# One written-out order on all five engines for the attention of two batches

## The chip, the cores and the metric

The kernel runs on one core of a Trainium2 chip. A core has five engines that work at the same time, each with an instruction list of its own that it takes in order: TensorE (matrix products, PE), VectorE (DVE), ScalarE (ACT, activation functions and copies), GpSimd (POOL) and SyncE (SP, which here only issues transfers). ACT and POOL issue transfers too. An instruction waits for semaphores that other engines or transfers raise; while it waits, everything behind it on its list waits as well. All transfers share 16 DMA engines. The metric is device time in microseconds (us); all data is float32.

## The reference

Four batches of 512 tokens with 512 channels pass through an attention block and a feed-forward block, each behind a layer norm whose shift, scale and output gate come from a small modulation product.

```python
mod = (silu(c) @ wmod).reshape(4, 6, 1, 512)
sa, ca, ga, sb, cb, gb = (mod[:, i] for i in range(6))
ga, gb = ...                                  # sign kept, magnitude at least 0.25
h = layernorm(x) * (1 + ca) + sa
x = x + ga * attention(h)
h = layernorm(x) * (1 + cb) + sb
x = x + gb * ((silu(h @ w_gate.T) * (h @ w_up.T)) @ w_down.T)   # 2048 hidden channels

def attention(h):                             # 6 heads, key size 64, value size 128
    q, k, v = (silu(conv4(h @ W)) for W in (Wq, Wk, Wv))        # causal, 4 taps
    beta = sigmoid(h @ Wb)
    g = -exp(A_log) * softplus(h @ Wa + dt_bias)
    q, k = l2norm(q) / 8, l2norm(k)
    for t in tokens:                          # gated delta rule, state S of 64 x 128 per head
        S = S * exp(g[t])
        S = S + outer(k[t], (v[t] - k[t] @ S) * beta[t])
        o[t] = q[t] @ S
    o = o * rsqrt(mean(o * o) + 1e-5) * norm_weight * silu(h @ Wg)
    return o @ Wo
```

## The kernel before

**Stages.** Tokens are cut into 4 tiles (`NT`) of 128 per batch, each of two chunks of 64. For each batch `normed_t` makes the normed, modulated and transposed input `ht` (DVE statistics and scaling, TensorE transposes, an ACT pass with shift and scale). Then come 18 projections per batch, 128 output channels each: 3 of keys, 3 of queries, 6 of values, 6 of gates. A projection is four accumulating products of 512 columns into one PSUM bank (each is two instructions in the trace, since the data is float32). Keys, queries and values go through `conv_silu` (L427): ACT copies the bank with the last tap's weight (L432), DVE adds three taps (L434), ACT applies silu (L438). Keys and queries are also squared (L444) and summed over channels by TensorE (`pn`, L450); values are transposed and scaled (`by_token`, L496); gates only get a silu. All four results are stored to DRAM (`kd`, `qd`, `vd`, `sd`) and read back later in another layout. `decays` and `stored` make the decay factors from two small products (`pab`, `pat`).

**The delta rule.** `triangles(b)` makes, for all chunks and heads of a batch at once, the inverse of the 32 x 32 unit triangles: 30 pairs of DVE instructions in a chain (L598, L602), results to DRAM as `td` and `ttd`. For each tile `operands` loads keys, queries, values and triangles, builds the matrices `l`, `yk` and `it` (TensorE into the bank pair `scratch`, DVE and ACT out of it), and `scan` carries the state over the two chunks: `pf` (L695), a copy on ACT (L700), `pm` (L704), copies on DVE and ACT (L711, L712). `finish` and `project` norm and gate the output, multiply with `wo` (L745), add the residual, store `xmid` and take the second norm; `turned` transposes it into `hf`, the input of `feed_forward`.

**The rest.** `modulation(j)` makes one of six modulation vectors. `weight_sums` makes sums of feed-forward weights, 16 times a load, four POOL instructions (L808 to L811) and a store from POOL's queue (L812), through one buffer. `feed_forward(b)` multiplies with these sums (L960) and with `w_down` (L847, L890).

**What sets the order.** The program text calls the stages one after the other, and a planner that is part of the framework moves instructions past each other on every engine, by its own estimates of cost, as far as data and buffers allow; for all but batch 0 it is told that the inverse chain is of low priority (`LATER`, L594). `lagging` (L413) and `between` put a few pieces later in the program text by hand. The text issues batch 0's projections, its triangles and its delta rule, then the keys and queries of batches 1 to 3 together, and so on; batch 2's triangles and both delta rules of batches 2 and 3 are issued beside the feed-forwards. PSUM has three banks tagged `fill` (projections), three tagged `seq` (delta rule and small products) and the pair `scratch`. SP issues nearly all loads and stores, ACT the stores of `kd`, `qd` and `sd`, POOL those of the weight sums and of the output gates.

Of the kernel before, what the change touches and what calls it, by code (L numbers as in the profile page):

```python
# [7 lines left out]

F32 = mybir.dt.float32
AF = mybir.ActivationFunctionType  # L10
ALU = mybir.AluOpType
# [26 lines left out]
def adaln_block(  # L38
# [119 lines left out]
    act.activation(warm, eps, AF.Silu)  # L158
    act.activation(sc_t[:, :, :B], c_in, AF.Silu)

    last, steps = [], []

    def between(i):

        if i % 2 and steps:
            steps.pop(0)()


    def after(t):

        pool.tensor_copy(t, last[0][:1, :1])

    def modulation_load(j):

        early = j < 2
        wm = pa_.tile([P, KD, D], F32, tag="ht" if early else "wm", bufs=3 if early else 1, name=f"wm{j}")
        if not early:
            after(wm[:1, 0, :1])
        (act if early else sp).dma_start(
            wm, w_mod[:, j * D : (j + 1) * D].rearrange("(k p) f -> p k f", p=P)  # L180
        )
        return j, wm

    def modulation(j, wm):

        pm = fill(f"pm{j}")
        for k in range(KD):
            pe.matmul(pm[k * S : (k + 1) * S, :], sc_t[:, k, :], wm[:, k, :], start=True, stop=True)
        part = pa_.tile([P, D], F32, tag="acc", bufs=4, name=f"part{j}")
        vec.tensor_copy(part, pm)  # L190
        if j in MOD:
            pt = fill(f"pmt{j}")[:, : KD * B].rearrange("p (t b) -> p t b", b=B)
            for t in range(KD):
                pe.matmul(pt[:, t, :], part[:, t * P : (t + 1) * P], fold[:, :B], start=True, stop=True)
            vec.tensor_scalar_add(mod_t[:, MOD[j]], pt, 1.0 if j in (1, 4) else 0.0)
            return
        pg = fill(f"pmg{j}")[:B, :]
        pe.matmul(pg, fold[:, :B], part, start=True, stop=True)
        val = pa_.tile([P, D], F32, tag="acc", bufs=4, name=f"val{j}")[:B]
        vec.tensor_copy(val, pg)  # L200
        mag = pa_.tile([P, D], F32, tag="acc", bufs=4, name=f"mag{j}")[:B]
# [4 lines left out]
        pool.dma_start(gate_d[j // 3], mag)  # L206
# [6 lines left out]
    def load_x(b):  # L213
        ts = []
        if b == 2:

            room = w1.tile([P, NT, D], F32, tag="hf", bufs=2, name=f"xt{b}")
        for c in range(NT):
            if b == 2:
                t = room[:, c, :]  # L220
            else:
                t = pa_.tile([P, D], F32, tag="xt", bufs=4, name=f"xt{b}_{c}")
            (act if b else sp).dma_start(t, x[b, c * P : (c + 1) * P, :])
            ts.append(t)
        return ts

    for j in (1, 0):
        modulation(*modulation_load(j))
    first_w = weight(w_k, 0, "k0_0")
    xts = load_x(0)  # L230
# [4 lines left out]
    for nm, src, n in (("k", conv_k, NP), ("q", conv_q, NP), ("v", conv_v, H)):  # L235
        cw[nm] = const.tile([P, n, TAPS], F32, name=f"conv_{nm}")
        sp.dma_start(cw[nm], src.rearrange("(n p) i -> p n i", p=P))
    neg_a = const.tile([P, H], F32, name="neg_a")
    sp.dma_start(neg_a, a_log.partition_broadcast(P))
    act.activation(neg_a, neg_a, AF.Exp)  # L240
    pool.tensor_scalar(neg_a, neg_a, -1.0, None, ALU.mult)
    dtb = const.tile([P, H], F32, name="dtb")
    sp.dma_start(dtb, dt_bias.partition_broadcast(P))
    nw = const.tile([P, 1], F32, name="nw")
    sp.dma_start(nw, norm_weight.rearrange("(p o) -> p o", o=1))
    for t in gd:
        for a in range(2):
            sp.dma_start(t[a, 0, :, :, 0:1], far)
# [30 lines left out]
    def normed_t(b, xts):  # L279

        ht = pa_.tile([P, KD, T], F32, tag="ht", bufs=3, name=f"ht{b}")
        mv = pa_.tile([P, NT, vec.BN_AGGR_DIM], F32, tag="mv", name=f"mv{b}")
        rstd = pa_.tile([P, NT], F32, tag="rstd", name=f"rstd{b}")
        for c in range(NT):
            statistics(pa_, xts[c], mv[:, c, :])
        act.activation(rstd, mv[:, :, 1], AF.Sqrt, bias=eps)
        vec.reciprocal(rstd, rstd)
        for c in range(NT):
            vec.tensor_scalar(
                xts[c], xts[c], mv[:, c, 0:1], rstd[:, c : c + 1], ALU.subtract, ALU.mult  # L290
            )
        for k in range(KD):
            pt = fill(f"pxt{b}_{k}")
# [6 lines left out]
        return ht  # L300

    def decays(bs, hts):
# [3 lines left out]
        pab = (seq if bs == [0] else fill)(f"pab{n}")  # L321
# [18 lines left out]
        pat = (seq if bs == [0] else fill)(f"pat{n}")  # L340
# [18 lines left out]
        act.activation(beta, pv[:, :, :, H : 2 * H].rearrange("p b c h -> p b h c"), AF.Exp, scale=-1.0)  # L359
        flat = [v.rearrange("p b h c -> p (b h c)") for v in (z, e, t, t2, s, beta)]  # L360
        fz, fe, ft, ft2, fs, fb = flat
        vec.tensor_scalar_add(fb, fb, 1.0)
        vec.reciprocal(fb, fb)


        vec.scalar_tensor_tensor(fe, fz, -1.0, fz, ALU.mult, ALU.max)
        act.activation(fe, fe, AF.Exp, scale=-1.0)
# [3 lines left out]
        vec.tensor_mul(ft2, ft, ft)  # L371
        vec.tensor_scalar_mul(fs, ft2, 1.0 / 17.0)
        for q in (15.0, 13.0, 11.0, 9.0, 7.0, 5.0, 3.0):
            vec.scalar_tensor_tensor(fs, fs, 1.0 / q, ft2, ALU.add, ALU.mult)
        vec.scalar_tensor_tensor(fs, fs, 1.0, ft, ALU.add, ALU.mult)
# [8 lines left out]
        return beta, lambda: stored(bs, m, n, gy, g, y)  # L384

    def stored(bs, m, n, gy, g, y):

        pd = (seq if bs == [0] else fill)(f"pd{n}")
# [10 lines left out]
        for i, b in enumerate(bs):  # L399
# [3 lines left out]
            pgt = (seq if bs == [0] else fill)(f"pgt{b}")  # L403
# [3 lines left out]
            act.dma_start(  # L407
                gd[b].rearrange("a g h c i -> (g h c) a i")[:, :, 1:],
                gyt.rearrange("p (a i) -> p a i", a=2),
            )  # L410

    tails, pending = [], []

    def lagging(tail=None, lag=2):

        if tail is not None:
            tails.append(tail)
        while len(tails) > (lag if tail is not None else 0):
            tails.pop(0)()

    def projected(w, ht, nm):
        pp = fill(f"pp_{nm}")
        for k in range(KD):
            pe.matmul(pp, w[:, k, :], ht[:, k, :], start=(k == 0), stop=(k == KD - 1))  # L424
        return pp

    def conv_silu(w, taps, col, ht, nm):  # L427

        pp = projected(w, ht, nm)
        acc = pa_.tile([P, T], F32, tag="acc", bufs=4, name=f"acc_{nm}")  # L430
        last[:] = [acc]
        act.activation(acc, pp, AF.Copy, scale=taps[:, col, TAPS - 1 : TAPS])  # L432
        for i in range(1, TAPS):
            vec.scalar_tensor_tensor(  # L434
                acc[:, i:], pp[:, : T - i], taps[:, col, TAPS - 1 - i : TAPS - i], acc[:, i:],
                ALU.mult, ALU.add,
            )
        act.activation(acc, acc, AF.Silu)  # L438
        return acc

    def squares(t, dst, p, scale, nm):

        sq = pa_.tile([P, T], F32, tag="sq", bufs=1, name=f"sq_{nm}")
        act.activation(sq, t, AF.Square)  # L444
# [10 lines left out]
    def keys(bs, hts):  # L455
        if bs == [0]:
            betas, store = decays(bs, hts)
        sk = {}
        for i, b in enumerate(bs):
            sk[b] = pa_.tile([P, H, NT], F32, tag=f"sk{i}", bufs=1, name=f"sk{b}")  # L460
        for p in range(NP):
            w = first_w if bs == [0] and p == 0 else weight(w_k, p, f"k{bs[0]}_{p}")
            for b in bs:
                n = f"k{b}_{p}"
                kt = conv_silu(w, cw["k"], p, hts[b], n)
                act.dma_start(kd[b][:, p, :], kt)
                lagging(lambda a=(kt, sk[b], p, 1.0, n): squares(*a))
            if p == 1 and bs != [0]:
                betas, store = decays(bs, hts)
            if p == (1 if bs == [0] else 2):  # L470
                store()
        def scalars():
            for i, b in enumerate(bs):
                act.activation(nk[b], sk[b], AF.Sqrt)
                pool.tensor_scalar(nk[b], nk[b], -1.0, None, ALU.mult)
                vec.reciprocal(sc[b], sk[b])
                vec.scalar_tensor_tensor(sc[b], sc[b], -1.0, betas[:, i], ALU.mult, ALU.mult)

        lagging(scalars)

    def queries(bs, hts):
        for p in range(NP):
            w = weight(w_q, p, f"q{bs[0]}_{p}")
            for b in bs:
                n = f"q{b}_{p}"
                qt = conv_silu(w, cw["q"], p, hts[b], n)
                act.dma_start(qd[b][:, p, :], qt)
                lagging(lambda a=(qt, eq[b], p, float(DK) * EPS, n): squares(*a))

    def values(bs, hts):  # L490
        for h in range(H):
            w = weight(w_v, h, f"v{bs[0]}_{h}")
            for b in bs:
                vt = conv_silu(w, cw["v"], h, hts[b], f"v{b}_{h}")
                lagging(lambda a=(b, h, vt): by_token(*a))
                between(h)  # L496

    def by_token(b, h, vt):
# [8 lines left out]
        sp.dma_start(vd[b][:, :, h, :].rearrange("c p v -> p c v"), v)  # L507

    def gates(bs, hts):
        for h in range(H):  # L510
            w = weight(w_g, h, f"g{bs[0]}_{h}")
# [609 lines left out]
```

## Time and profile before

| what | us |
|---|---|
| median of 3 runs | 1313.92 (1313.06 to 1315.52) |
| span of the profiled execution | 1315.2 |
| TensorE busy in it | 1234.9 |
| VectorE / ScalarE / GpSimd busy | 733.7 / 383.5 / 290.8 |
| first key product starts | 23.9 |
| last product of batches 0 and 1 up to the second norm | 537.6 |
| first product of the feed-forward | 522.0 |

Busy time counts instructions, overlaps within an engine once. PEclk is the share of TensorE's full clock that was granted; at half clock a product takes twice as long and still counts as busy. The chain of waits goes back from the last instruction to what released each step. "PE a <- ACT b: 9.7, 4, 5.8" says that TensorE waited 9.7 us in all, 4 times, at most 5.8, for b on ScalarE.

### The profile page before, as it was taken

Reading aid. Unit: us, or ns where it says so; the run is one execution under the profiler, and the core shown is the slowest. Engines: PE = TensorE matmul, PEld = TensorE weight load, DVE = VectorE, ACT = ScalarE, POOL = GpSimd, SP = SyncE. Lnnn points to the kernel's source line nnn. Section 1 sums busy time; section 2 is a strip of 40 time slices with the busy share of each in tenths; the row PEclk is TensorE's granted clock in tenths of the full one; section 3 lists DMA queues with packets and bytes.
Section 4 is the critical chain, followed back from the end, with each engine's and each line's share of the span. In section 5 each row is a group of like instructions: output and inputs, shape, how many; then the busy total and the mean of one; then the engine's idle time right before and its main releaser. Section 6 shows DMA issues by size and latency. Waiting matters only on the chain.

```text
span 1315.2 us, 18413 instructions
## 1 busy us (share of the span) xinstructions
PE 1234.9 (94%) x6752; PEld 807.1 (61%) x6752; DVE 733.7 (56%) x1574; ACT 383.5 (29%) x740; POOL 290.8 (22%) x357
## 2 busy tenths in 40 slices
PE   6799898999889998999999999799999999999998
PEld 3345355554344565767757666666666578888884
DVE  3665865656188255784445558543555543563564
ACT  2633355554142354211103332101134312112110
POOL 4100214533210012030023121233111221131113
PEclk9799898999899999999999999899999999999999
DMA  7579667667874537664436555544632555444431
GB/s 209 138 203 288 186 173 209 172 212 249 255 205 126 144 98 176 199 202 139 134 113 189 124 126 165 161 130 150 193 85 70 174 186 175 146 152 152 140 114 62
DMA packets 217945, 214.57 MB, mean 163 GB/s; under 512 B 95608, under 2 KB 164216, under 8 KB 217856
## 3 DMA queue, kind: packets, MB, share of 16 engines
q1 hardware_dynamic: 194976, 176.58, 46.4%
q10 hardware_dynamic: 19360, 17.93, 4.2%
q0 software_dynamic: 3520, 18.89, 3.8%
q8 instruction: 54, 0.88, 0.3%
q14 instruction: 35, 0.29, 0.1%
HBM read 159.23 MB, written 50.97 MB: 160 GB/s over the span
## 4 chain that ended last, share of the span: by engine, by line
PE 64%; DVE 14%; DMA 11%; POOL 5%; issue 3%; ACT 2%; SPq 1%; POOLq 0%; DVEq 0%; ACTq 0%
PE phg L960 14%; PE phu L960 11%; PE pd L847 9%; PE pwo L745 5%; PE pds L890 4%; PE pp_v L424 3%; PE pp_g L424 3%; PE pm L704 2%; DVE ti L602 2%; PE scratch L631 2%; DMA wsum<-wsg 2%; DVE tip L598 2%; DMA wsum<-wsu 2%; PE pp_q L424 1%; PE pp_k L424 1%
## 5 line engine op out<-in xcount | busy, mean ns | idle before, releaser
L847 PE MATMUL pd<-wdn,hid 128*128 128x512 f32 x320 | 140.6, 592 | 0.0
L960 PE MATMUL phg<-hf,wg 128*128 128x256 f32 x512 | 138.4, 387 | 1.8 <-DMA wg<-wsum 1.8
L960 PE MATMUL phg<-hs,wg 128*128 128x256 f32 x384 | 103.6, 390 | 5.9 <-DVE hid L967 5.8
L960 PEld LDWEIGHTS phg<-hf,wg 128*128 128x128 f32 x512 | 95.9, 192 | 20.7 <-issue 6.3
L960 PE MATMUL phu<-hf,wu 128*128 128x256 f32 x384 | 101.1, 388 | 2.2 <-DMA wu<-wsum 2.0
L847 PEld LDWEIGHTS pd<-wdn,hid 128*128 128x128 f32 x320 | 60.7, 190 | 68.1 <-issue 63.6
L960 PE MATMUL phu<-hs,wu 128*128 128x256 f32 x384 | 95.6, 382 | 2.5 <-DVE up L973 2.5
L424 PE MATMUL pp_g<-ht,wg 128*128 128x512 f32 x192 | 91.6, 617 | 5.7 <-DMA wg<-in_w_g_dram 4.6
L853 POOL TENSOR_TENSOR xm<-xm,tmpf 128x512 f32<-128x512 f32 x40 | 50.9, 1273 | 206.8 <-DVE tmpf L852 206.8
L424 PE MATMUL pp_v<-ht,wv 128*128 128x512 f32 x192 | 89.3, 609 | 3.5 <-DVE v L503 2.3
L745 PE MATMUL pwo<-wo,ot 128*128 128x512 f32 x192 | 91.8, 608 | 0.0
L965 ACT COPY hid<-phg 128x256 f32<-128x256 f32 x32 | 11.9, 372 | 247.9 <-PE phg L960 247.9
L960 PEld LDWEIGHTS phg<-hs,wg 128*128 128x128 f32 x384 | 71.5, 193 | 20.4 <-DVE hid L967 8.3
L960 PEld LDWEIGHTS phu<-hs,wu 128*128 128x128 f32 x384 | 71.9, 191 | 19.2 <-DVE up L973 7.1
L960 PEld LDWEIGHTS phu<-hf,wu 128*128 128x128 f32 x384 | 71.7, 192 | 15.5 <-issue 3.1
L424 PEld LDWEIGHTS pp_g<-ht,wg 128*128 128x128 f32 x192 | 35.1, 195 | 43.0 <-issue 41.8
L852 DVE TENSOR_TENSOR tmpf<-pd,gb 128x512 f32<-128x512 f32 x40 | 27.5, 689 | 59.4 <-PE pd L847 44.7
L424 PEld LDWEIGHTS pp_v<-ht,wv 128*128 128x128 f32 x192 | 35.2, 193 | 41.5 <-issue 38.5
L989 ACT ACTIVATE hid<-hid 128x1024 f32<-128x1024 f32 x32 | 33.8, 1057 | 86.2 <-DVE hid L973 70.0
L434 DVE SCALAR_TENSOR_TENSOR acc_v<-pp_v,conv_v,acc_v 128x511 f32<-128x511 f32 (+2 forms) x72 | 53.4, 743 | 9.8 <-ACT acc_v L432 8.8
L704 PE MATMUL pm<-r,l 128*128 128x128 f32 x384 | 53.8, 285 | 1.0 <-ACT r L700 0.9
L704 PEld LDWEIGHTS pm<-r,l 128*128 128x128 f32 x384 | 48.2, 194 | 8.9 <-ACT r L700 4.7
(244 smaller groups left out, 2060.1 us busy)
## 6 DMA issues: line engine op xcount, KB each, us to landing
wdn<-in_w_down_t_dram SPq DMA_DIRECT2D x32, 512.0 KB, 4.3
wg<-wsum SPq DMA_DIRECT2D x32, 512.0 KB, 3.8
wu<-wsum SPq DMA_DIRECT2D x32, 512.0 KB, 3.6
wg<-wsum SPq DMA_DIRECT2D x32, 384.0 KB, 4.4
wu<-wsum SPq DMA_DIRECT2D x32, 384.0 KB, 4.3
wsum<-wsg POOLq DMA_DIRECT2D x8, 896.0 KB, 4.3
wsum<-wsu POOLq DMA_DIRECT2D x8, 896.0 KB, 4.6
vd<-v SPq DMA_DIRECT2D x24, 256.0 KB, 3.4
```

Of the source, the lines that this page charges most:

```text
L424: pe.matmul(pp, w[:, k, :], ht[:, k, :], start=(k == 0), stop=(k == KD - 1))
L434: vec.scalar_tensor_tensor(acc[:, i:], pp[:, : T - i], taps[:, col, TAPS - 1 - i : TAPS - i], acc[:, i:], ALU.mult, ALU.add,)
L598: vec.tensor_tensor(v, pm[:, j, j + 1 :, None].broadcast_to([n, m, j]), t[:, j : j + 1, :j].broadcast_to([n, m, j]), ALU.mult,)
L602: vec.tensor_add(t[:, j + 1 :, :j], t[:, j + 1 :, :j], v)
L704: pe.matmul(pm[:, h], l[:, hs.start + h, 2 * par : 2 * par + 2, :], r[:, par, hs.start + h], start=True, stop=True,)
L745: pe.matmul(pw, ot[:, h, :], wo[:, h, :], start=(h == 0), stop=(h == H - 1))
L847: pe.matmul(pd, hids[q, i // 2][:, i % 2, c * P : (c + 1) * P], wdn[q, i // 2][:, i % 2, :], start=(i == 0), stop=(i == NQ - 1),)
L852: vec.tensor_mul(tmp, pd, gb)
L853: pool.tensor_add(xm[c], xm[c], tmp)
L890: pe.matmul(o[:, c], l[:, c * P : (c + 1) * P], r, start=j == 0, stop=j == 1)
L960: pe.matmul(o, l[:, k], r[:, k], start=k == 0, stop=k == 1)
L989: act.activation(hid, hid, AF.Silu)
```

## The change

From the opening to the end of the last projection the planner no longer orders anything: the instructions of this part are issued on all five engines as the program text has them. The text itself is rewritten around a list of 72 projection units; each has two half steps, numbered 0 to 143, and everything else is cut into pieces that are put at a numbered half step. What comes after (feed-forwards, delta rules of batches 2 and 3, triangles of batch 3) is still planned, but behind the last instruction of the written part on each engine.

The order of the units changes: keys and queries of batch 0 (units 0 to 5), gates of 0 and 1 (6 to 17), values of 0 (18 to 23), keys of 1 and 2, then 3 (24 to 32), queries (33 to 35) and values (36 to 41) of 1, gates of 2 (42 to 47), queries of 2 and 3 (48 to 53), values of 2 and 3 (54 to 65), gates of 3 (66 to 71). The three inverse chains are spread over half steps 26 to 37, 84 to 95 and 132 to 143, where gates are projected; the triangles of batch 2 move into the written part. The tiles of the delta rules start every 8 half steps from 48 (batch 0) and 96 (batch 1).

```diff
+    def opening():
+        loads = [(j, modulation_load(j)) for j in (1, 0)]
+        act.activation(warm, eps, AF.Silu)
+        act.activation(sc_t[:, :, :B], c_in, AF.Silu)
+        act.activation(warm, eps, AF.Sqrt)
+        idle = seq("idle")
+        for i in range(24):
+            pe.transpose(idle[:, (i % 4) * P : (i % 4 + 1) * P], ident, ident)
...
+        for c in (0, 2, 1, 3):
+            if c < 2:
+                vec.tensor_scalar(
+                    xts[c], xts[c], mv[:, c, 0:1], rstd[:, c : c + 1], ALU.subtract, ALU.mult
+                )
+            else:
+                act.activation(
+                    xts[c], xts[c], AF.Identity, bias=off[:, c : c + 1], scale=rstd[:, c : c + 1]
+                )
...
+    def put(h, *fns):
+        side.setdefault(h, []).extend(fns)
+    def spread(gen, hs):
+        for h in hs:
+            put(h, lambda: next(gen, None))
...
+    def far_stores():
+        for t in gd:
+            for a in range(2):
+                pool.dma_start(t[a, 0, :, :, 0:1], far)
+    put(6, far_stores)
+    spread(decays([0]), [1, 2, 3, 4, 4, 5, 6, 7, 8, 10])
...
+    def inverse(b, prepared, first):
+        spread(tri[b], prepared)
+        spread(tri[b], [first + 2 * i // 5 for i in range(S - 2)])
+        spread(tri[b], [first + 12, first + 13])
...
+    inverse(2, [116, 117, 118, 119, 121, 122, 124, 126, 127, 128, 129, 130, 132], 132)
+    for j, h in ((2, 12), (3, 20), (4, 28), (5, 36)):
+        spread(modulation(j), [h, h + 5, h + 7, h + 8, h + 10])
...
+    def windows(b, h0):
+        for c in range(NT):
+            h = h0 + 8 * c
...
+            put(h, lambda c=c: kq(b, c, 0))
+            put(h + 1, lambda c=c: kq(b, c, 1))
+            put(h + 3, lambda c=c: kq(b, c, 2))
+            put(h + 5, lambda c=c: cross(b, c))
+            put(h + 6, lambda c=c: cross_t(b, c))
+            put(h + 7, lambda c=c: decayed(b, c))
+            h += 8
+            put(h, lambda c=c: solve(b, c, 0))
+            put(h + 2, lambda c=c: step(b, c, 0))
+            put(h + 4, lambda c=c: solve(b, c, 1))
+            put(h + 6, lambda c=c: step(b, c, 1))
...
+            if h >= 2 * len(units):
+                pending.append(lambda c=c: (to_model(b, c, range(4, H)), x_to_hf(b, c)))
+                continue
...
+    windows(0, 48)
+    windows(1, 96)
+    for i in range(NF // 2):
+        for (w, hs) in (
+            ((w_gate_t, wsum[0], "g"), (-1, 1, 2)), ((w_up_t, wsum[1], "u"), (3, 5, 6))
+        ):
+            spread(weight_sums(i, *w), [56 + 8 * i + h for h in hs])
+    with tc.manual_schedule(engines=engines):
+        opening()
...
+        for u in range(n + 2):
+            while queue and queue[0][1][0] <= u + 3:
+                i, (_, src, p, nm) = queue.pop(0)
+                ws[i] = weight(src, p, f"{nm}{i}")
+            for half in range(2):
+                if u < n:
+                    nm, p, b, wi = units[u]
+                    if not half:
+                        pps[u] = fill(f"pp_{nm}{b}_{p}")
+                    for k in (2 * half, 2 * half + 1):
+                        pe.matmul(
+                            pps[u], ws[wi][:, k, :], hts[b][:, k, :], start=(k == 0), stop=(k == KD - 1)
+                        )
+                prev = units[u - 1] if 0 < u <= n else None
+                if prev and not half:
...
+                        act.activation(acc, pp, AF.Copy, scale=t[:, p, TAPS - 1 : TAPS])
+                        for i in range(1, TAPS):
+                            vec.scalar_tensor_tensor(
+                                acc[:, i:], pp[:, : T - i], t[:, p, TAPS - 1 - i : TAPS - i],
+                                acc[:, i:], ALU.mult, ALU.add,
+                            )
+                halfway(2 * u + half)
...
+                        squares_sum(sqs.pop(u - 2), sk[b], p, 1.0, f"k{b}_{p}")
...
+                if prev and prev[0] != "g":
+                    nm, p, b, _ = prev
+                    acc = accs[u - 1]
+                    act.activation(acc, acc, AF.Silu)
+                    if nm != "v":
+                        act.dma_start((kd if nm == "k" else qd)[b][:, p, :], acc)
+                        sq = pa_.tile([P, T], F32, tag="sq", bufs=1, name=f"sq_{nm}{b}_{p}")
+                        act.activation(sq, acc, AF.Square)
+                        sqs[u - 1] = sq
+    last_of = {}
+    for ins in nc.cur_bb.bb.instructions:
+        if ins.engine in engines:
+            last_of[ins.engine] = ins
     stage_a.close()
     pc_ = ctx.enter_context(tc.tile_pool(name="pc", bufs=2, reuse_waits="tile"))
+    for e in last_of.values():
+        rest.enter_context(tc.issue_after(e))
...
-    triangles(2)
     feed_forward(0)
     delta_rule(2)
```

`halfway(h)` calls the pieces that were put at half step h. Smaller edits go with it: the bodies of `operands`, `scan`, `finish` and `project` become functions of one step each (`kq`, `cross`, `cross_t`, `decayed`, `solve`, `step`, `o_means`, `gated`, `to_model`, `residual` and others); in `layer_norm` of batches 1 to 3 ACT does the scaling that DVE did; copies out of PSUM in `modulation` go from DVE to ACT; the weight sums and output gates are stored from SP, the eight `far` values from POOL; the squares of the outputs go into the spent tile `r`.

## The prediction

> **What bounds it now.** I read the busy table and the 40 slices first, then the busy time in two stretches, before and after 538 us, where the last product of the two attention batches ends, then who waited for whom on TensorE, and last the order of time around that border.
>
> ```profile
> span 1315.2 us, 18413 instructions
> PE 1234.9 (94%) x6752; PEld 807.1 (61%) x6752; DVE 733.7 (56%) x1574; ACT 383.5 (29%) x740; POOL 290.8 (22%) x357
> PE   6799898999889998999999999799999999999998
> PEclk9799898999899999999999999899999999999999
> ```
> TensorE is the bound over the whole run, and its holes and low clocks stand in the first 17 slices, the part that the change rewrites.
>
> ```profile
> 0.00:538.00 538.00, 484.44 (x2918) 258.89 (x2919) 308.41 (x674) 217.44 (x388) 120.41 (x185) 0.96 0.67 189
> 538.00:1315.00 777.00, 750.49 (x3836) 548.24 (x3834) 425.26 (x901) 166.08 (x352) 170.36 (x172) 0.99 0.47 146
> 30.00:60.00 30.00, 21.05 (x81) 9.86 (x80) 22.60 (x61) 19.04 (x26) 1.52 (x3) 0.73 0.55 138
> 330.00:360.00 30.00, 25.35 (x118) 11.32 (x117) 2.77 (x4) 3.80 (x7) 6.75 (x10) 0.89 0.85 265
> ```
> The columns are the stretch, its length, then busy us of PE, PEld, DVE, ACT and POOL, the granted clock, the DMA share and GB/s. Up to 538 TensorE idles 538 - 484.4 = 53.6 us, and of its busy time 484.4 x 0.04 = 19 us is lost to the clock. No other engine is near full there (DVE 57%, ACT 40%). So at most 73 us can be won here. After 538 it idles 27 us in code that stays.
>
> ```profile
> PE pn_k L450 <- ACT sq_k L444: 9.7, 4, 5.8
> PE pm L188 <- DMA wm<-in_w_mod_dram: 6.5, 1, 6.5
> PE pmt L194 <- DVE part L190: 4.9, 4, 3.5
> PE pp_g L424 <- DMA wg<-in_w_g_dram: 4.6, 1, 4.6
> PE pxn L762 <- DVE xn L756: 3.7, 5, 2.3
> ```
> The 53.6 us are many small waits of different kinds: the engines' orders do not fit each other, and no single resource is short.
>
> **The work that stays.** Of the 484.4 us, 465 are left at full clock. Before 538 the feed-forward of batch 0 has already run 28 products of 256 columns, at 4 in 0.86 us: 6 us. So the stage holds 459 us of TensorE work and really ends at 532. From below: 72 projection units of 8 instructions at 0.43 us (18 took 7.97) are 248; a chunk of the delta rule is two solves of 0.88, two steps of 2 x 0.8, three kq of 0.72, cross, its transpose and the decayed product 0.92 + 0.90 + 1.13, gating 1.1, output 5.3, last transpose 0.6, in all 17, eight times 136; norm sums and value transposes 48 x 0.6 = 29; x transposes 11, decays 11, three triangles 6, four modulations about 13; less what falls due behind the loop (2.4), about 447 after the opening of some 11. Both ways agree, so no TensorE work of weight is removed. What changes is when it runs.
>
> **The change part by part.**
> Opening. Both modulation loads now issue at once (the second left at 6.42), the eight far stores leave SP (5.12 + 3.00 us of issue, ahead of wab and the later wk), and the normalising is split between DVE and ACT. Chain: first product ends near 9.2, part copied 0.7, four statistics of 0.85, sqrt, reciprocal and offset 1.0, two normalisings of about 0.7 on each engine, last transposes and batch 0's shift near 20, first key product at 20.3, where before it stood at 23.9 behind 1.5 us of pab. Bounds 18 and 24. The 24 added transposes (5.6 us at the 0.23 of pxt) lie in the hole before 6.5 and may hold the first product 0.8 us, which is in the 9.2. The granted clock reads 1.00 up to 40 us and 18 key products took 7.97 us from 28.55, so I give the warm-up nothing.
>
> Key and query units 0 to 5. In ACT's written order the copy of unit u stands behind the square of unit u-1, so this is a ring: copy 0.68, three taps 2.23, silu 0.63, the issue of the store 0.41, square 0.62, hops 0.3: 4.9 us a unit against 4.07 of TensorE. Two switches to exp and back stand in it where DVE's result comes late, 3.4 us each. 6 x 4.9 + 6.8 = 36; bounds 27 (TensorE alone) and 42 (23.9 to 65.8 before).
> Before, an activation began 0.01 us after a 1.28 us table load (33.84, 35.13). [...]
>
> Units 6 to 23: gates of batches 0 and 1, values of 0. TensorE 84 us. DVE has no taps in the gates, and the chain of 30 pairs (0.15 to 0.40 us each, 18 us in all, 1.5 us a half step) lies beside 1.7 to 2.3 us of TensorE per half step; it ends 8 half steps before the first load of its result. DMA has to bring some 22 MB meanwhile (weights 4.5, gates and values out 4.5, modulation 4, x 2, wo 1.5, triangle 4.7, chunk loads 0.8), 262 GB/s; the slice above shows 265 with the share at 0.85. I add 4; bounds 0 and 20 (22 MB at 204 GB/s).
>
> Units 24 to 71, with both delta rules. TensorE 336 us; DVE 250 (taps 36 x 2.23, chunks 8 x 11.6, value scalings 18 x 0.7, two triangles 27 each, decays and norms about 10); ACT some 175; POOL 89: 2.6 us of DVE under 3.5 of TensorE in a half step. Each step of a chunk has one or two half steps between producer and consumer, and sqrt of two chunks shares one table switch. The 16 weight sums, a chain of some 10 us each before, get 4 half steps (14 us); their stores and the 16 waits of the next load for the landing (4.3 to 4.6 us) now stand on SP. Queued behind such a wait are weights wanted three units later (20 us), chunk loads two half steps later and value stores: covered. Without that cover each costs up to 4 us. I add 10 us of small stalls; bounds 0 and 37 (the 90% of the old stage). Clock 3 (0 to 8). Sum: 20.3 + 36 + 88 + 346 + 3 = 493.
>
> Handover. This is new, and it costs. SP's written list ends with the stores of inverse 2, behind its last copy (1.04 us) at the end of the loop, and the feed-forward's loads come after it. Before, they went out in the middle of the delta rule's tail:
>
> ```profile
> 504.81 1.59 SPq L819 DMA_DIRECT2D gb<-gate_d  x1
> 506.45 3.75 SPq L823 DMA_DIRECT2D xm<-xmid  x4
> 510.31 0.39 SPq L981 DMA_DIRECT2D wdn<-in_w_down_t_dram  x1
> 510.86 0.39 SPq L950 DMA_DIRECT2D wg<-wsum  x1
> 537.58 0.63 PE L762 MATMUL pxn<-ident,xn 128*128 128x128 f32 x4 [2.34 <-DVE xn L756]
> ```
> Six us of issues stand ahead of the first wg, and it lands 3.8 to 4.4 us after its issue, while 27 us of tail covered it; gates 3 and the tail of batch 1 now end together. Copy, issues and landing make 8 to 12 us; I take 8.5, as the xm issues have less to wait for, and 3 for the clock: after the 5.8 us hole at 48 it stayed at 0.50 until 60. Bounds 5 and 15.
>
> Feed-forward starts at 493 + 11.5 = 504.5, with 2.4 us of tail still to run, against 532: 25 us saved. Taking inverse 2 off DVE there (27.9 of 30 us busy at 540) is worth 0 to 2.5; I take 1. The profiled span becomes 1315.2 - 26 = 1289; the median of the runs lay 1.3 below the span, so 1288.
>
> **Rivals.**
> Stalls at the head of the list, the slower one. With one order, a side product that waits holds every projection behind it. Place: the 96 half steps of the delta rules. My 10 us are 0.1 us a half step; from 0.37 on (10 + 26 over 96) the change loses. At 0.5 it is 48 us and 1326. For it: the waits of pn_k, pxn and pot show such hand-offs arriving 1 to 6 us late. Against: one half step of 3.5 us lies between, and no engine but TensorE is over 75%.
> DMA under the gates. At 204 GB/s the gates cost 20 us instead of 4: 1304. For: the wg wait of 4.6 us. Against: 228 GB/s held from 60 to 150 with TensorE at 91%.
> Nearly ideal: units 0 to 5 at 28, no DMA stall, 2 us lost in the delta rules, handover 5: 26 us more, 1262. Against: the ring and the handover follow from the order as written.
> That the order isn't kept: the five queues issue in order and nothing is left to a planner up to the border, so I give this none.
>
> **How the numbers follow.** Forecast 1288 with 0.57 (its own range 1270 to 1303), DMA 0.12, nearly ideal 0.09, head-of-list stalls 0.22. A difference of 0.2% (2.6 us) is about what this measurement can tell from no change. Faster takes the first three less a few hundredths of long DMA stalls, 0.75; same 0.04; slower 0.21. The range goes from 1264, which holds most of the nearly ideal case, to 1320, where the slower rival has 0.43 us a half step.
>
> **What would show it.** First key product at 18 to 24 us; the first gate product near 57, with TensorE waiting for sq_k or acc_k before it; granted clock 1.00 from there to the border; TensorE busy 94 to 98% in the delta rules; no TensorE wait for a weight sum; the first phg near 505, after a hole of 5 to 12 us released by DMA wg; the rest of the feed-forward 775 to 785 us long. The prediction fails if TensorE's idle time in the delta rules is over 36 us, or if the feed-forward, whose order is still planned, comes out over 10 us longer or shorter.

## The result and the profile after

The changed kernel takes 1398.23 us (1397.06 to 1401.55, 4 runs) against 1314.72 for the kernel before beside it: a ratio of 1.0642, 95% interval 1.061 to 1.0674. It is slower by 6.4%. The profiled execution has a span of 1399.8 us at a mean granted clock of 0.932, against 1315.2 and 0.977.

The page of the changed kernel, its busy table and two of its 40 rows of slices:

```profile
span 1399.8 us, 18425 instructions
PE 1251.3 (89%) x6776; PEld 826.4 (59%) x6776; DVE 742.0 (53%) x1559; ACT 391.8 (28%) x758; POOL 283.5 (20%) x342
...
PE   7896989898999997999999999999807968999998
...
PEclk9998989899999998999999999999955888999999
```

The first 16 slices, the rewritten part, are no better filled than before. The new thing stands in slices 30 to 34: there is a slice without any product, and the clock falls to half. That is 1015 to 1190 us, far behind the written part, in code that is still planned.

Busy time by stretch (the columns as in the prediction): opening and units 0 to 5, units 6 to 23, units 24 to 71, the handover, the feed-forward.

```profile
0.00:52.00 52.00, 40.43 (x204) 21.62 (x205) 23.43 (x61) 23.76 (x37) 18.32 (x60) 0.93 0.66 199
52.00:156.00 104.00, 88.52 (x372) 40.28 (x372) 55.28 (x131) 42.71 (x64) 4.35 (x5) 0.90 0.64 181
156.00:531.00 375.00, 343.24 (x2319) 190.89 (x2320) 246.16 (x511) 163.45 (x306) 89.03 (x104) 0.95 0.70 196
531.00:547.00 16.00, 7.09 (x34) 4.19 (x32) 14.11 (x21) 6.26 (x11) 6.86 (x4) 0.72 0.90 303
547.00:1399.00 852.00, 771.99 (x3851) 569.38 (x3850) 402.99 (x838) 155.67 (x342) 164.91 (x169) 0.93 0.39 128
```

The feed-forward's first product stands at 547.1 and not at the 504.5 of the forecast, a loss of 42.6 us; from there to the end it takes 852.7 us where the forecast had 784.7, a loss of 68. Together that is the 110.6 us between 1289.2 and 1399.8. The larger part lies in code of which the forecast said that it stays.

TensorE's order of time in that hole:

```profile
1006.16 1.46 PE L998 MATMUL pds<-wdn,hid 128*128 128x256 f32 x6
1007.55 0.68 PE L549 MATMUL scratch<-kp 64*64 64x64 f32 x28
...
1016.51 1.22 PE L641 MATMUL scratch<-qc,kc 64*128 64x128 f32 x8 [1.19 <-DVE yk L652]
1053.45 1.57 PE L663 MATMUL scratch<-t,at 64*64 64x32 f32 x24 [35.72 <-DMA t<-td]
```

At 1007.6 the last feed-forward product that can run is done. Only then come the products that prepare batch 3's triangles (`kp`), and the delta rule waits 35.7 us for the result of the chain (`td`). Meanwhile VectorE waits 6.6 us for the chain's input and then runs the chain; from 1020 to 1050 us TensorE, ScalarE and GpSimd do nothing. The store of batch 3's `td`, first in the kernel before, then in the changed one:

```profile
833.97 0.34 SPq L606 DMA_DIRECT2D td<-ti  x1
```

```profile
1048.25 0.31 SPq L586 DMA_DIRECT2D td<-ti  x1
```

One change in the diff can have moved it; the first two lines below stood round the 30 pairs of the chain alone:

```diff
-        with tc.high_priority(-LATER if b else 0):
-            for j in range(1, S - 1):
...
+    def triangles(b):
+        with tc.high_priority(-LATER):
+            for _ in triangle_steps(b):
+                pass
```

The body of `triangles` became a generator, so that it can be dealt out over half steps, and the low priority went round the loop that drives it. For batch 3, the one that the planner still places, it now covers the loads, scans, products and stores too, and not the chain alone. Experiments 1 and 2 test this.

### The profile page after: what moved, and what is told of

Same layout as the page of the kernel before. It is cut to its first block, busy times and chain, and to the rows that moved or that the text cites. A ratio compares the mean times of both kernels' runs of the same rounds, so it can differ in the third digit from the quotient of the medians.

```text
span 1399.8 us, 18425 instructions
## 1 busy us (share of the span) xinstructions
PE 1251.3 (89%) x6776; PEld 826.4 (59%) x6776; DVE 742.0 (53%) x1559; ACT 391.8 (28%) x758; POOL 283.5 (20%) x342
## 4 chain that ended last, share of the span: by engine, by line
PE 66%; DVE 17%; DMA 5%; issue 4%; ACT 4%; POOL 2%; SPq 1%; ACTq 0%; POOLq 0%; DVEq 0%
PE phg L1068 14%; PE phu L1068 11%; PE pd L955 9%; PE pds L998 4%; PE pwo L799 4%; PE pp_v L1275 4%; PE pp_g L1275 2%; DVE ti L580 2%; PE pm L729 2%; DVE tip L576 2%; PE pp_k L1275 2%; PE pp_q L1275 2%; PE scratch L641 2%; PE pf L714 2%; PE scratch L686 1%
## 5 line engine op out<-in xcount | busy, mean ns | idle before, releaser
L1068 PEld LDWEIGHTS phg<-hf,wg 128*128 128x128 f32 x512 | 97.1, 192 | 20.3 <-issue 6.1
L1275 PE MATMUL pp_v<-ht,wv 128*128 128x512 f32 x192 | 98.9, 647 | 3.0 <-issue 2.2
L799 PE MATMUL pwo<-wo,ot 128*128 128x512 f32 x192 | 94.6, 620 | 0.9 <-DVE ot L791 0.8
L729 PEld LDWEIGHTS pm<-r,l 128*128 128x128 f32 x384 | 53.5, 212 | 17.6 <-ACT r L719 8.2
L729 PE MATMUL pm<-r,l 128*128 128x128 f32 x384 | 58.5, 304 | 5.4 <-ACT r L719 5.3
L799 PEld LDWEIGHTS pwo<-wo,ot 128*128 128x128 f32 x192 | 35.6, 196 | 38.7 <-issue 34.2
```

Source lines behind the costliest of these rows:

```text
L729: pe.matmul(pm[:, h], l[:, hs.start + h, 2 * par : 2 * par + 2, :], r[:, par, hs.start + h], start=True, stop=True,)
L799: pe.matmul(st[b, c]["pw"], st[b, c]["ot"][:, h, :], wo[:, h, :], start=(h == 0), stop=(h == H - 1))
L1068: pe.matmul(o, l[:, k], r[:, k], start=k == 0, stop=k == 1)
L1275: pe.matmul(pps[u], ws[wi][:, k, :], hts[b][:, k, :], start=(k == 0), stop=(k == KD - 1))
```

## The experiments

Ratios are to the kernel before, run beside each set: it took 1315.8 us beside experiments 1 to 4, 1317.2 beside 5 to 7 and 1316.6 beside 8 and 9. Intervals are of 95%.

**1. The block drawn narrow again.** The changed kernel, with this edit:

```diff
-    def triangle_steps(b):
+    def triangle_steps(b, low=0):
...
         for j in range(1, S - 1):
+            with tc.high_priority(low):
...
     def triangles(b):
-        with tc.high_priority(-LATER):
-            for _ in triangle_steps(b):
-                pass
+        for _ in triangle_steps(b, -LATER):
+            pass
```

> The changed kernel with the lowered priority drawn round the thirty steps of batch 3's inverse chain alone, as the kernel before had it, instead of round the whole of batch 3's triangles; nothing else. Theory A (the wide block sends batch 3's preparation, and with it the delta rule of batch 3, to where no feed-forward products are left to fill its waits): the feed-forward part, from the first gate half product to the end, goes back from 852 us to the 783 us of the kernel before, so 1398 - 68 = 1330 us, range 1322 to 1340, and TensorE's wait of 35.7 us for the t load is gone. Rival B (the planner starts the feed-forward from wrong times, because of the written-out part and the edges from its last instructions, whatever the priority): 1390 to 1402 us.

Measured: 1322.25 us, ratio to before 1.0044 (1.0016 to 1.0073). Theory A holds, B falls. The stretches from 1020 to 1080 us, of the changed kernel and then of this one:

```profile
1020.00:1050.00 30.00, 0.00 (x0) 0.00 (x0) 21.67 (x63) 0.00 (x0) 0.00 (x0) 0.50 0.13 33
1050.00:1080.00 30.00, 22.83 (x196) 18.43 (x198) 5.83 (x15) 6.44 (x17) 0.00 (x0) 0.50 0.22 48
```

```profile
1020.00:1050.00 30.00, 28.28 (x121) 18.04 (x120) 14.46 (x31) 10.58 (x22) 5.59 (x4) 1.00 0.31 104
1050.00:1080.00 30.00, 30.00 (x111) 20.44 (x110) 14.43 (x28) 4.46 (x8) 7.83 (x8) 1.00 0.69 237
```

The first set has TensorE at 0 us of 30 and then busy at half clock; in the second there is no hole and the clock stays at 1.00. The gain is 76 us and not 68: the feed-forward from its first product on now takes 1320.6 - 548.1 = 772.5 us, 10.7 less than the 783.2 that the kernel before took from 532.0 on. The first product itself is no earlier than in the changed kernel (548.1 against 547.1), so this block has no part in the loss ahead of it.

**2. The wide block alone, in the kernel before.**

```diff
-    def triangles(b):
+    def triangle_body(b):
...
-        with tc.high_priority(-LATER if b else 0):
+        with tc.high_priority(-LATER if b and b != 3 else 0):
             for j in range(1, S - 1):
...
+    def triangles(b):
+        with tc.high_priority(-LATER if b == 3 else 0):
+            triangle_body(b)
```

> The kernel before, with only the wide block added: all of batch 3's triangles at the lowered priority, not the chain alone. Theory A: the same 68 us come out as a loss without any written-out order, so 1314 + 68 = 1382 us, range 1365 to 1395, with TensorE waiting 20 to 36 us for the t load of batch 3 and the delta rule of batch 3 late in the trace. Rival B: no loss, 1314 us within 5.

Measured: 1402.73 us, 1.0655 (1.0605 to 1.0705), 87 us more: theory A's mechanism, and 8 us over its range; B falls. First the longest wait of TensorE, then its row of slices:

```profile
PE scratch L664 <- DMA t<-td: 40.5, 3, 35.9
```

```profile
PE   6799899998999999989999999999915878999998
```

The same wait of 36 us and a slice at one tenth, without a written order anywhere. So this block alone costs the kernel before about as much as the whole change does; by experiment 1 the rest of the change costs 0.4%.

**3. One load earlier.** In the written part of the changed kernel TensorE had two longest holes after the opening: 6.5 us for `o`, of which experiment 5 speaks, and 6.3 us that end at 136.6 us. What led to the second, on SyncE, VectorE, ScalarE and TensorE in the changed kernel:

```profile
93.47 9.03 SPq L222 DMA_DIRECT2D xt<-in_x_dram  x4
102.61 0.36 SPq L565 DMA_DIRECT2D pm<-ad  x1
106.65 1.03 DVE L569 COPY ti<-pm 96x1024 f32<-96x1024 f32 x1 [21.62 <-DMA pm<-ad]
135.95 0.63 ACT L1314 ACTIVATE acc_v<-acc_v 128x512 f32<-128x512 f32 x1
136.63 1.11 PE L485 MATMUL pvt<-ident,acc_v 128*128 128x128 f32 x4 [6.32 <-ACT acc_v L1314]
```

The load `pm` of batch 0's chain and batch 3's x loads share half step 24, and the x loads come first and take 9 us, while their tiles come free. VectorE stands 21.6 us at the chain's first copy; the chain then runs where the first value taps should, and they reach ScalarE at 136.

In the kernel of experiment 1 this hole is 8.6 us long. The edit to that kernel:

```diff
-    spread(norms[3], [24, 34, 35, 38, 40, 41, 48, 49, 50, 51])
+    spread(norms[3], [27, 34, 35, 38, 40, 41, 48, 49, 50, 51])
```

> The narrow block of the first experiment, and batch 3's four x loads moved from half step 24 to half step 27, so that the queue reaches the load of batch 0's chain first. Theory C (the hole at 120 to 136 us is one late load: it went out at 102.6 us behind x loads that waited, and the chain then stood in VectorE's list before the first value taps): the load goes out near 91 us, the chain ends by 122 us, the hole of 6.3 us at the first transposed value and the stretch at clock 0.83 go, 8 to 12 us less than the first experiment, so about 1320 us (1316 to 1324). Rival D (VectorE's own backlog in these half steps holds the value taps, whenever the chain's data come): within 3 us of the first experiment, 1327 to 1333.

Measured: 1311.21 us, 0.9962 (0.994 to 0.9983): 11 us less than experiment 1, so C and not D; the time lies under C's range of 1316 to 1324, which had been counted from 1330 us for experiment 1. It is now 0.4% under the kernel before. In its trace, SyncE and VectorE:

```profile
93.24 0.30 SPq L565 DMA_DIRECT2D pm<-ad  x1
...
97.58 1.05 DVE L569 COPY ti<-pm 96x1024 f32<-96x1024 f32 x1 [13.91 <-DMA pm<-ad]
```

The chain starts 9.1 us earlier than in the changed kernel, the hole at the first transposed value is gone, and the first product of batch 1's keys comes at 144.4 us instead of 156.3.

**4. The opening without its transposes.** From the changed kernel:

```diff
-        idle = seq("idle")
-        for i in range(24):
-            pe.transpose(idle[:, (i % 4) * P : (i % 4 + 1) * P], ident, ident)
```

> The changed kernel without the 24 transposes that run at the start into a bank that nobody reads. Theory W (they bring TensorE up to speed, and the opening is shorter for it): the first modulation product takes 1.9 us again instead of 1.06, and the first key product starts 1 to 3 us later than 18.5 us; the whole 1399 to 1402 us. Rival (the opening waits for the second modulation weight and for the x rows anyway): the first product is slower but the key product starts at 18.5 us within 0.5, and the time is 1398 us within 1.

Measured: 1394.62 us, 1.0596 (1.0557 to 1.0635), an interval that overlaps that of the changed kernel. The time lies under both expectations. TensorE at the start, with the transposes and then without:

```profile
6.79 1.06 PE L173 MATMUL pm<-wm,sc_t 128*32 128x512 f32 x8 [0.38 <-DMA wm<-in_w_mod_dram]
...
12.25 1.89 PE L173 MATMUL pm<-wm,sc_t 128*32 128x512 f32 x8 [2.48 <-DMA wm<-in_w_mod_dram]
```

```profile
6.75 1.94 PE L173 MATMUL pm<-wm,sc_t 128*32 128x512 f32 x8 [6.75 <-DMA wm<-in_w_mod_dram]
...
12.12 1.94 PE L173 MATMUL pm<-wm,sc_t 128*32 128x512 f32 x8 [0.70 <-DMA wm<-in_w_mod_dram]
...
18.49 2.84 PE L1272 MATMUL pp_k<-ht,wk 128*128 128x512 f32 x6 [0.54 <-ACT ht L476]
```

The first product does gain 0.9 us from them, but the opening then waits 2.5 us for the second modulation weight, and behind that hole the second product takes 1.89 us, nearly the 1.94 of the opening without them. The first key product stands at 18.5 either way: the rival is right on that. The last run repeats this on the best kernel.

**5. Three places in the delta rules.** From the kernel of experiment 3:

```diff
-    inverse(1, [68, 69, 70, 71, 73, 76, 77, 78, 79, 80, 81, 82, 84], 84)
+    inverse(1, [68, 71, 72, 73, 75, 76, 77, 78, 79, 80, 81, 82, 84], 84)
...
-    spread(decays(list(range(1, B))), [53, 55, 57, 58, 58, 59, 59, 65, 66, 67, 68, 73, 74, 75])
+    spread(decays(list(range(1, B))), [53, 55, 57, 58, 58, 59, 62, 65, 66, 67, 68, 73, 74, 75])
...
-            put(h + 2, lambda c=c: o_normed(b, c))
+            side.setdefault(h + 2, []).insert(0, lambda c=c: o_normed(b, c))
...
-            ((w_gate_t, wsum[0], "g"), (-1, 1, 2)), ((w_up_t, wsum[1], "u"), (3, 5, 6))
+            ((w_gate_t, wsum[0], "g"), (-1, 2, 3)), ((w_up_t, wsum[1], "u"), (3, 5, 6))
```

> The last kernel (narrow block, x loads at 27) with three places of the written order moved, each ahead of a wait that its trace shows: the decay products of batches 1 to 3 from half step 59 to 62 (TensorE waited 6.0 us for gy), the scans of batch 1's triangles from 69-71 to 71-73 and their exponentials from 73 to 75 (VectorE stood 7.2 us at the scan whose load had not landed, and TensorE 4.1 us behind it), the normalization of o put ahead of the other operations of its half step, and the sums of the gate weights one half step behind it (TensorE waited 6.8 us for o). Theory E (the stage's shortfall is heads of lists that wait, and each wait goes when its place is moved): 6.0 + 4.1 + 5.0 = 15 us off 1311, so 1296 us, range 1290 to 1303, and the three rows gone from the table of waits. Rival F (the engines behind are full, so that the wait turns up at the next instruction): within 4 us of 1311.

Measured: 1307.39 us, 0.9931 (0.9904 to 0.9958), some 4 us instead of 15, which is F's number; the interval overlaps that of experiment 3, so even these 4 us are not clear of noise. TensorE's waits from 52 to 516 us, first in the kernel of experiment 3, then here:

```profile
PE pot L790 <- POOL o L781: 8.8, 2, 6.8
PE scratch L686 <- ACT lm L677: 7.6, 4, 4.1
...
PE pd L383 <- DVE gy L375: 6.0, 1, 6.0
```

```profile
PE scratch L686 <- ACT lm L677: 8.4, 3, 6.7
...
PE scratch L641 <- DVE yk L652: 5.2, 3, 2.9
PE pxn L862 <- DVE xn L829: 4.5, 2, 3.2
PE pvt L485 <- ACT acc_v L1314: 3.0, 1, 3.0
```

The row for `gy` has gone, that for `o` has gone down to 0.6 us, and new ones have come. Where the 6.7 us come from is seen two experiments on.

**6. The tail of the written part.** The changed kernel leaves the end of batch 1's last tile (the last residual and second norm) to the planner. In the kernel of experiment 3, batch 3's scans (running sums of the decay exponents, `ec`) and the products with them stood in front of the last residual at the handover. VectorE, then GpSimd:

```profile
518.52 3.50 DVE L511 TENSOR_TENSOR_SCAN ec<-ec,start 128x520 f32<-128x520 f32 x3
521.94 1.48 DVE L941 TENSOR_TENSOR hs<-hf 128x512 f32<-128x512 f32 x1
523.34 0.68 DVE L807 TENSOR_TENSOR tmpa<-pwo,ga 128x512 f32<-128x512 f32 x1
...
520.56 5.20 POOL L520 TENSOR_TENSOR ec<-ec,sc 128x512 f32<-128x512 f32 x3 [11.13 <-ACT ec L516]
525.73 1.70 POOL L808 TENSOR_TENSOR xr<-xr,tmpa 128x512 f32<-128x512 f32 x1
```

Without these lines that end is written out like the others:

```diff
-            if h >= 2 * len(units):
-                pending.append(lambda c=c: (to_model(b, c, range(4, H)), x_to_hf(b, c)))
-                continue
```

> The kernel with the narrow block and the x loads at 27, and the end of the last window of batch 1 (residual, statistics, second norm, its turning) in the written order too, instead of left to the planner, which put batch 3's scans, its products on GpSimd of 5.2 us and the four differences of the feed-forward in front of it. Theory G (these stand on the path at the handover): the first gate half product at 527 us instead of 533.25, TensorE's wait of 8.7 us for yk gone or under 3 us, so 1311 - 6 = 1305 us, range 1301 to 1308. Rival H (the differences, now behind the norm, hold the third half product instead): no gain within 3 us, 1308 to 1314.

Measured: 1308.38 us, 0.9944 (0.9917 to 0.9971), 3 us less than experiment 3 and not clear of noise. H's number, but not its mechanism. SyncE and TensorE:

```profile
516.63 2.64 SPq L931 DMA_DIRECT2D xm<-xmid  x2
521.28 0.32 SPq L811 DMA_DIRECT2D xmid<-xr  x1
521.65 0.94 SPq L931 DMA_DIRECT2D xm<-xmid  x2
523.17 0.41 SPq L1058 DMA_DIRECT2D wg<-wsum  x1
...
530.50 2.05 PE L1068 MATMUL phg<-hf,wg 128*128 128x256 f32 x4 [5.31 <-DMA wg<-wsum]
```

The norm is done at 523.5, but the weights have only just been asked for: in SyncE's list they stand behind the loads of `xmid`, and these behind its last store.

**7. Both sets together.** The edits of experiments 5 and 6 in one kernel.

> Both sets of edits together. Theories E and G: they lie in different stretches, so the gains add, 1311 - 15 - 6 = 1290 us, range 1283 to 1298, and 1.6 to 2.3% under the kernel before. Rivals F and H: 1304 to 1314 us.

Measured: 1306.03 us, 0.9913 (0.9881 to 0.9945): the rivals' range. The long wait of experiment 5 is there again. SyncE, VectorE, TensorE:

```profile
410.10 2.84 SPq L909 DMA_DIRECT2D wsu<-in_w_up_t_dram  x4
412.98 1.12 SPq L502 DMA_DIRECT2D ec<-gd  x2
...
418.94 1.24 DVE L511 TENSOR_TENSOR_SCAN ec<-ec,start 128x520 f32<-128x520 f32 x1 [9.78 <-DMA ec<-gd]
...
426.42 0.91 PE L686 MATMUL scratch<-lm,yk 64*64 64x64 f32 x12 [6.45 <-ACT lm L677]
```

The store of the gate sums, one half step later, lets the up weights load later through the one buffer, and behind that load on SyncE stands the `ec` load for batch 2's scans: VectorE waits 9.8 us for it (4.3 us in the kernel of experiment 3), the copies of the delta rule behind it, and TensorE for these. So the edits that took 6.8 us away made 6.5 elsewhere.

**8. The new heads of lists moved too.** Batch 2's scans two half steps later, and for batch 0 the loads of `gb` and `xm`, now in a function `load_xm`, behind the feed-forward's first block:

```diff
-    inverse(2, [116, 117, 118, 119, 121, 122, 124, 126, 127, 128, 129, 130, 132], 132)
+    inverse(2, [116, 119, 120, 121, 122, 123, 124, 126, 127, 128, 129, 130, 132], 132)
...
+        if b:
+            load_xm()
...
+            if b == 0 and i == 0:
+                load_xm()
```

> The kernel with both sets of edits, and two more: the scans of batch 2's triangles from half steps 117-119 to 119-121 (in the trace VectorE stood 9.8 us at the first of them, whose load went out late behind loads of the weight sums, and TensorE 6.4 us behind it), and the first loads of the feed-forward's weights ahead of its loads of xmid, which are needed only at the first down products (the weights' load went out at 520.98 us behind them; TensorE's first half product began at 528.14). Theory E: the new waits were the moved heads of lists, so 6.4 and about 4.5 us go, 1306 - 11 = 1295 us, range 1288 to 1301. Rival F (they turn up again at the next instruction): 1302 to 1308 us.

Measured: 1298.63 us, 0.9857 (0.9829 to 0.9886): theory E's range. 1.4% under the kernel before, the best of the study. The two edits were not run apart. Its trace is of the fastest of five executions (1292.4 us), some 6 us under their median. The handover in it, TensorE:

```profile
504.01 3.60 PE L799 MATMUL pwo<-wo,ot 128*128 128x512 f32 x8
511.93 1.08 PE L862 MATMUL pxn<-ident,xn 128*128 128x128 f32 x4 [4.32 <-DVE xn L829]
...
515.78 2.07 PE L1071 MATMUL phg<-hf,wg 128*128 128x256 f32 x4 [2.04 <-DMA wg<-wsum]
```

From the end of the last output product to the first half product it is 8.2 us, against 13.0 in the changed kernel. TensorE's longest wait for `lm` fell from 6.5 to 1.2 us.

**9. The best one without the transposes.**

> The same without the 24 transposes at the start. If these cost time (without them the changed kernel took 1394.6 us against 1398.2, and the clock of the first 52 us read 0.97 against 0.93): 1 to 4 us less than with them. If that difference was chance: within 1 us of it.

Measured: 1300.89 us, 0.9882 (0.9857 to 0.9908), 2.3 us more and not less; the two intervals overlap, and the sign is the opposite of experiment 4. The first key product stands at 20.0 us here and at 18.5 in experiment 8, but over the seven traces with the transposes it varies from 18.3 to 20.3. The transposes have no effect that these runs can tell from none.

## Why the prediction was wrong

**The step that failed** is "After 538 it idles 27 us in code that stays", and with it "the rest of the feed-forward 775 to 785 us long". The call of `triangles(3)` stayed where it was, but the block around its body did not. It was in the diff, and I read the new generator for its half steps only. The runs showed in its place a TensorE wait of 35.7 us and a feed-forward of 852.7 us; with the block narrow again 76 us went (experiment 1), and the block alone cost the kernel before 87 us (experiment 2). No rival had it: the 1326 of the head-of-list rival is near the 1322 of experiment 1, but the 76 us on top come from elsewhere. The test that the prediction named for its own failure, the feed-forward over 10 us longer, is the one that struck.

This step alone would not have saved the forecast: with the block narrow the time is 1322.3 us, still 34 over it. In the changed kernel the first feed-forward product comes 42.6 us late, and these are terms of the sum:

**Opening** 20.3: measured 18.5, inside its bounds. "I give the warm-up nothing" came out as its price, though not as its reason: there is a slow start (1.94 against 1.06 us for the first product), hidden by the second weight.

**Units 0 to 5**, 36: measured 51.9 - 18.5 = 33.4. The ring held: from one silu to the next it is 4.7 to 5.0 us where no table is switched, against the 4.9 worked out. ScalarE's table load at 24.50 us takes 1.28 us, begins 0.02 us after the activation ahead of it ends and is followed by the next one after 0.01 us.

**Units 6 to 23**, 84 + 4: measured 104. The 4 us were meant for transfers, which ran at 181 GB/s with a share of 0.64, under the 283 GB/s with a share of 0.87 that the same trace has from 330 to 360 us; that is 18.8 MB in 104 us and not 22. (At 204 GB/s 22 MB take 24 us more than the 84, and not 20 as the bound and the rival have it.) The term that I had not made was the queue: that the `pm` load stands behind x loads which wait for their tiles, and what stands behind the chain on VectorE. "It ends 8 half steps before the first load of its result" was about the wrong reader. Experiment 3 gives back 11 us.

**Units 24 to 71**, 346 and 3 for the clock: measured 375. TensorE idled 375 - 343.2 = 31.8 us, where I had 10, under the 36 that I had named as failure; and of its busy time 343 x 0.05 = 17 us went to the clock, where I had 3 for everything. The mechanism is the head-of-list rival's, and half of the idle time stands in a few long waits (6.8, 6.0 and 4.1 us in the kernel of experiment 3), not in the even loss of 0.1 us a half step that I took. The clock's loss stands beside them: these waits end at 335, 192 and 248 us, and the stretches 300 to 350, 156 to 200 and 200 to 250 are granted 0.93, 0.85 and 0.94, against 1.00 from 350 to 400, where no wait is over 1.4 us. Four instructions of a projection take 3.62 and 3.78 us shortly behind the first two, and 1.88 at 340 and 184 us. From experiment 3 to the trace of experiment 8 this part goes from 373 to 360 us, TensorE's idle time in it only from 32.5 to 28.2, and the clock from 0.95 to 0.99. In these traces a long wait goes with a low clock on top of its own length, where the prediction expected 1.00 from the first gate product on. Experiments 5 to 8 show too that a wait does not simply go away when its place is moved.

**Handover**, 11.5: measured 547.1 - 530.7 = 16.4, over its upper bound of 15. SyncE's part came as worked out (the store of `td` at 531.4, the first wg at 537.3), but the last to come was another: the residual behind batch 3's scans and products.

**Feed-forward**, with 1 us for taking batch 2's chain off it: with the block narrow it is 10.7 us shorter than in the kernel before, and most of this doesn't stand beside the chain. Behind 532 us the kernel before had 2.4 us of tail left, which the prediction names, and a wait of 2.3 us for the last norm; it waited 3.8 us for two loads of weight sums between 700 and 900 us. The only wait of TensorE for VectorE beside the chain is 2.5 us. No run took the chain away alone, so its price stays open.

The count from below has a slip as well: its terms as listed add up to 452 and not 447. It cost nothing: busy time times clock gives 80 and 326 us for the two long stretches, where the sum has 84 and 336.

With experiment 8 the written order reaches 1298.6, 11 us above the forecast. What is left there is for the most part in TensorE's waits for `xn` (the second norm), `lm` and `yk` (matrices of the delta rule), 8.8, 8.9 and 6.8 us in all and each 1 to 4 us long; these were not tried.

## What to carry to other kernels

When a diff turns a function into pieces, look at every scope that surrounds its call: a priority that covered one loop may now cover its inputs and outputs, and its price is paid far from the edit, where a later stage has lost the work that filled its waits. In a written order, price each load that must wait for a buffer with all that stands behind it on its queue, and then with all that stands behind its reader; in this case half of TensorE's idle time was there, and not in an even loss per step. When one is moved, look at what its queue does next before counting the gain.

## What the runs showed of the hardware

The granted clock does not show the slow start: in the stretch of 6 to 8 us it reads 1.00 in both openings, while eight instructions of the same product take 1.94 us without the transposes ahead and 1.06 behind them. It does show the slow second product behind the hole of 2.5 us in the changed kernel (1.89 us, 0.59 from 12 to 14 us); in the opening without transposes it reads 1.00 there too, at 1.94 us. The 24 transposes, 4.67 us that end 0.38 us before it, left the first product at nearly twice the speed; why, the traces don't show.

Four VectorE operations with two operands in SBUF (on-chip memory) took longer beside GpSimd. The four differences of the feed-forward took 0.68, 0.67, 0.68 and 0.68 us where GpSimd was idle (experiment 7); beside its `ec` products and the residual (experiment 3) they took 1.48, 0.93, 1.52 and 1.74. `tmpa`, with one operand in PSUM, took 0.68 beside the same `ec` products. What makes the four longer, these rows don't show.
